# A block-attention and layer-norm kernel: three pair tiles and two single banks in PSUM, whole copies of the weight parts, sums in the keys' bank, and a new order of steps

## The chip, the cores and the metric

The kernel runs on one core of a Trainium2 chip. The core has five engines with a queue of instructions each: TensorE (PE, matmuls, with PEld for its weight loads), VectorE (DVE), ScalarE (ACT), GpSimd (POOL) and SyncE (SP, which issues the DMAs here). SBUF holds operands in 128 partitions; PSUM, where matmuls write, has eight banks of 128 x 512 floats. The metric is the device time of one execution in microseconds (us); lower is better.

## The reference

For each of 8 batches x is 512 x 1024 (float32). It is cut into 8 blocks of 64 rows. With q the second row of cond:

```
block  = sums of the 64 rows of each block            # 8 x 1024
keys   = block @ Wk.T, divided by their RMS, times rms_weight
attn   = softmax over the 8 blocks of keys . q
p      = (attn-weighted sum of block) @ Wo.T          # one row per batch
y      = x + p
out    = x + (y - mean(y)) / sqrt(var(y) + 1e-6) * gamma + beta
```

The residual in the last line is the input x, before p is added.

## The kernel before, in words

The 8 batches are four **groups** of two. A group's x comes in four tiles of 128 partitions x 2 rows x 1024, so there are 32 **rows** of 128 x 1024, named k = 0 to 31, eight to a group. Thirteen SBUF slots (x0 to x12) hold x tiles and, early on, the parts of Wk and Wo.

Per group: bs adds the blocks with matmuls against a 0/1 matrix (L417); col transposes the sums into columns (blkT, DVE, L427); proj.0 and proj.1 multiply them by the transposed Wk and Wo (L461, L447), which gives the keys and the values; the softmax (sm) is a chain of small steps on ACT, DVE, POOL and one small matmul, "sums" (L484 to L504); vw weights the values (L518); p spreads them over the partitions with eight matmuls (L533); two copies of 512 columns bring p into the SBUF tile pb (ACT L236, DVE L238). For group 0 the weights are transposed first: each part T is eight 128 x 128 transposes (L402) and two copies.

Per row k: S (DVE, L634) forms x + p in place with its sum, Q (ACT, L636) its squares' sum; a **unit** U of four rows (two at the very end) makes standard deviations and their reciprocals on POOL (v, std, s2, sd2, rs; the last units partly on ACT and DVE) and transposes small vectors (st, L709), which a copy brings into lt. D (DVE, L734) writes (gamma + std) times the row into PSUM; R (TensorE, L720) adds the rank-one terms of mean, p and beta from lt and a table, two rows at a time; E (ACT, L749) evicts the sum, scaled by the reciprocal deviation, back into x; SP stores it. Rows 30 and 31 are evicted in halves of 512 columns, one on ACT (L759) and one on DVE (L760).

PSUM is four tiles of two banks each, t0 to t3; a step's bank i lies in tile i // 2. Rows, weight parts and p each take a whole pair; sums, projections, st and block sums a single bank. A framework puts semaphores between instructions that touch the same tile, and takes a tile as a whole: an instruction that reads one bank of t3 waits for the last write into the other.

The order of work is written out by hand: every step has a number, and the string ORDER gives the numbers in the order in which they are issued, with a letter (a, b: which of the step's engines) and, after a colon, the bank or slot. "f n:bank" puts n **filler** matmuls of zeros into a bank (L848, nothing reads them; they also set the bank for a later D, whose matmul accumulates); "z" the same without start. Each engine works its own queue in that order.

## Time and profile before

| | us |
|---|---|
| runs, median of 3 | 156.93 (155.94 to 157.63) |
| profiled execution, its own time | 155.66 |
| its span (first to last instruction) | 153.9 |
| PE / DVE / ACT / POOL busy | 119.3 / 101.9 / 92.7 / 52.9 |
| mean granted clock of TensorE | 0.91 of 2.4 GHz |

The span is what the trace covers; 1.76 us of the execution's own time lie around it. The busy times are shares of stages with different limits; fillers are counted in PE's. A timeline row gives the start of an instruction, its length, the line, the operation and, in brackets, how long its engine stood idle before it and who ended that. Lengths in the timeline overlap a little at their ends, so instructions in a row start closer together than their lengths.

### The profile page before, as it was taken

What the parts mean: (1) busy time and instruction counts of PE and PEld (TensorE: products, weight loads), DVE (VectorE), ACT (ScalarE), POOL (GpSimd) and SP (SyncE); (2) the same over time, 40 slices, a digit from 0 to 9 for tenths busy, and PEclk for the clock granted to TensorE, in tenths of its full rate; (3) what the DMA queues carried; (4) which work ended last, traced back from release to release, by engine and by line L of the source; (5) the groups of instructions that cost most, each with busy time, mean ns of one, the idle gap of its engine ahead of it and who ended that gap; (6) DMA issues with size and microseconds to landing.
All of it is one profiled execution on the core that took longest, in us unless ns stands there. A gap on an engine that the chain in (4) does not pass through costs nothing.

```text
span 153.9 us, 3136 instructions
## 1 busy us (share of the span) xinstructions
PE 119.3 (77%) x1209; PEld 59.1 (38%) x1218; DVE 101.9 (66%) x181; ACT 92.7 (60%) x156; POOL 52.9 (34%) x88
## 2 busy tenths in 40 slices
PE   5978465799988998997695888896496898469660
PEld 2548255369654653443342313432241222212110
DVE  3022250317419996598999999678939999966940
ACT  3054211125414996648999968688589769967620
POOL 6882000000000261602087282259209326960000
PEclk9999999999999999999999559999689559779955
DMA  5999999999999980065999706246240752546793
GB/s 132 421 394 428 424 408 408 409 422 416 420 418 424 404 358 17 4 271 182 424 349 400 292 2 277 87 185 272 102 170 9 321 228 100 243 204 272 321 360 136
DMA packets 7671, 42.77 MB, mean 278 GB/s; under 512 B 824, under 2 KB 824, under 8 KB 3816
## 3 DMA queue, kind: packets, MB, share of 16 engines
q1 hardware_dynamic: 7584, 42.54, 68.7%
q8 instruction: 9, 0.15, 0.4%
q14 instruction: 6, 0.05, 0.1%
q10 hardware_dynamic: 72, 0.04, 0.1%
HBM read 25.73 MB, written 16.78 MB: 276 GB/s over the span
## 4 chain that ended last, share of the span: by engine, by line
PE 30%; DVE 29%; DMA 16%; ACT 10%; issue 7%; POOL 5%; ACTq 0%; DVEq 0%
DVE x L634 13%; DMA x<-in_x_dram 13%; DVE t L734 10%; PE t L461 7%; PE t L720 6%; ACT x L749 4%; PE t L417 4%; PE t L402 4%; DMA tab<-in_L_cond_ln_beta_dram 3%; PE t L533 3%; PE t L848 3%; PE t L447 3%; ACT pb L236 2%; POOL urs L703 1%; ACT square L636 1%
## 5 line engine op out<-in xcount | busy, mean ns | idle before, releaser
L734 DVE SCALAR_TENSOR_TENSOR t<-gam,ustd,x 128x1024 f32<-128x1024 f32 x32 | 40.5, 1287 | 7.5 <-ACT x L749 4.8
L636 ACT ACTIVATE square<-x,tot 128x1024 bf16<-128x1024 f32 x32 | 36.7, 1148 | 2.6 <-DVE x L634 2.2
L634 DVE SCALAR_TENSOR_TENSOR x<-x,pb 128x1024 f32<-128x1024 f32 x32 | 38.0, 1221 | 0.1
L749 ACT ACTIVATE x<-t,urs 128x1024 f32<-128x1024 f32 x30 | 32.5, 1107 | 6.8 <-PE t L720 3.8
L720 PE MATMUL t<-tab,lt 32*128 32x512 f32 x128 | 26.9, 750 | 3.5 <-ACT square L636 1.5
L848 PE MATMUL t<-zeros 128*128 128x512 bf16 x57 | 20.8, 483 | 10.4 <-DVE vw L518 2.9
L688 POOL TENSOR_SCALAR stat<-tot 128x8 f32<-128x8 f32 (+1 forms) x8 | 6.5, 813 | 61.4 <-DVE x L634 56.2
L417 PE MATMUL t<-x,blk 128*32 128x256 f32 x256 | 18.0, 414 | 3.1 <-DMA x<-in_x_dram 2.5
L402 PE MATMUL t<-ident,x 128*128 128x128 f32 x128 | 16.4, 282 | 4.2 <-DMA x<-in_L_cond_Wk_dram 2.6
L402 PEld LDWEIGHTS t<-ident,x 128*128 128x128 f32 x128 | 15.3, 193 | 6.4 <-issue 4.0
L461 PE MATMUL t<-wkT,blkT 128*32 128x256 f32 x256 | 15.4, 382 | 1.1 <-DVE blkT L427 0.6
L848 PEld LDWEIGHTS <-zeros 128*128 128x128 bf16 x66 | 6.8, 115 | 23.6 <-issue 20.2
L238 DVE COPY wkT<-t 128x512 f32<-128x512 f32 x7 | 4.7, 689 | 14.0 <-PE t L402 13.9
L720 PEld LDWEIGHTS t<-tab,lt 32*128 32x128 f32 x128 | 7.4, 210 | 16.2 <-issue 6.1
L461 PE MATMUL t<-woT,blkT 128*32 128x256 f32 x192 | 12.0, 382 | 1.8 <-ACT x L749 0.9
L236 ACT COPY wkT<-t 128x512 f32<-128x512 f32 x9 | 5.0, 588 | 13.5 <-PE t L402 12.4
L236 ACT COPY woT<-t 128x512 f32<-128x512 f32 x9 | 5.0, 585 | 11.9 <-DVE woT L238 6.9
L683 POOL TENSOR_TENSOR ustd<-uv,halfs 128x4 f32<-128x4 f32 (+1 forms) x8 | 11.6, 1453 | 1.2 <-ACT uv L679 0.7
L703 POOL TENSOR_TENSOR urs<-uv,halfs 128x4 f32<-128x4 f32 (+1 forms) x8 | 11.7, 1467 | 0.0
L417 PEld LDWEIGHTS t<-x,blk 128*32 128x32 f32 x256 | 7.6, 115 | 10.7 <-issue 3.3
L238 DVE COPY woT<-t 128x512 f32<-128x512 f32 x7 | 4.7, 688 | 10.4 <-ACT woT L236 5.4
L461 PEld LDWEIGHTS t<-wkT,blkT 128*32 128x32 f32 x256 | 7.6, 109 | 8.5 <-issue 1.3
(79 smaller groups left out, 96.7 us busy)
## 6 DMA issues: line engine op xcount, KB each, us to landing
x<-in_x_dram SPq DMA_DIRECT2D x16, 1024.0 KB
out_dram<-x SPq DMA_DIRECT2D x14, 1024.0 KB
x<-in_L_cond_Wk_dram SPq DMA_DIRECT2D x4, 1024.0 KB
x<-in_L_cond_Wo_dram SPq DMA_DIRECT2D x3, 1024.0 KB
x<-in_L_cond_Wo_dram SPq DMA_DIRECT2D x2, 512.0 KB
out_dram<-x SPq DMA_DIRECT2D x2, 512.0 KB
out_dram<-x SPq DMA_DIRECT2D x4, 256.0 KB
gam<-in_L_cond_ln_gamma_dram SPq DMA_DIRECT2D x1, 512.0 KB
```

The lines of the kernel that those rows point to most:

```text
L236: nc.scalar.copy(dst, src)
L402: nc.tensor.transpose(flat(pair(part))[:, bass.ts(c, P)], tile_of(name)[:, e % RT, c::HC], ident)
L417: nc.tensor.matmul(bank(f"bs{n}")[32 * j : 32 * j + 32, :QU], blk[G["g"]], tile_of(name)[:, r, bass.ts(j, QU)], start=(t == 0 and r == 0), ...
L461: nc.tensor.matmul(bank(name)[32 * j : 32 * j + 32, :QU], b[:, c, :], w[:, c, j], start=(c == 0), stop=(c == HC - 1),)
L634: add(f"S{k}", [(DVE, 1.15)], lambda e: nc.vector.scalar_tensor_tensor(x_row(k), x_row(k), 1.0, pb[n], ALU.mult, ALU.add, accum_out=total) ...
L636: add(f"Q{k}", [(ACT, 1.28)], lambda e: nc.scalar.activation(square, x_row(k), AF.Square, bias=total, scale=-float(H), accum_out=ssq), rea ...
L683: add(f"{T} std", [(POOL, 0.5 + 0.16 * U)], lambda e: nc.gpsimd.tensor_tensor(std, v, halfs[:, :1].to_broadcast([P, U]), ALU.pow), reads=[ ...
L703: add(f"{T} rs", [(POOL, 0.5 + 0.16 * U)], lambda e: nc.gpsimd.tensor_tensor(rs, v, halfs[:, 1:].to_broadcast([P, U]), ALU.pow), reads=[V, ...
L720: nc.tensor.matmul(pair(f"row{k}")[:, h, :], lts[q % NST][lo : lo + 32, r // RT, :], tab_of(k)[0][lo : lo + 32, :], start=False, stop=True ...
L734: add(f"D{k}", [(DVE, 1.21)], lambda e: nc.vector.scalar_tensor_tensor(flat(pair(name)), gam, std, x_row(k), ALU.add, ALU.mult), reads=["g ...
L749: add(f"E{k}", [(ACT, 1.13)], lambda e: nc.scalar.activation(x_row(k), flat(pair(name)), AF.Identity, scale=rs), reads=[RS], writes=[xk(k) ...
L848: nc.tensor.matmul(banks[i // 2][:, i % 2, :], zeros, zeros[:, 0:1].to_broadcast([P, HALF]), start=start, stop=True, skip_group_check=True)
```

## The change

PSUM becomes three pair tiles (t0 to t2, banks 0 to 5) and two single ones (b0 and b1, banks 6 and 7). A step of the new kind "P" takes two banks that may lie in two tiles: p of each group, the weight part T1.7 and row 31. The other weight parts are copied by one instruction of 1024 columns. The softmax's sums go into columns 256 to 271 of the keys' bank, and that bank is held until the scores (sc) are taken. Row 31 has its own D, R and E per half; row 30 is evicted whole and stored as one piece. There is a filler of 256 columns ("h"). ORDER is new: the softmax of group 2 stands earlier, the scaling of gam goes to ACT, two more of the lt copies go to DVE, there are 81 fillers in place of 66, and two x tiles swap slots.

```diff
@@ -28,6 +28,7 @@
 FORMS = ('y',)
-SPLIT = (30, 31)
+SPLIT = (31,)
+APART = ((1, 7),)
 ALONE = (30, 31)
 UP = 32768.0
-SINGLE = (28, 29)
+SINGLE = (28, 29, 30)
 POOL_UNITS = (0, 1, 2, 3, 4, 5, 6, 7)
@@ -42,24 +43,24 @@
 ORDER = (
-    "1 3 45:0 84 2 4 0 46:1 87 75 5 86 47:2 6 82 7 48:3 8 9 10 11 12 14 13 15 16 17 18 19 20 21 22 23 24 f11:7 "
...
+    "1 3 45:0 84 2 4 75 46:1 92 5 0 79 47:2 6 80 7 48:3 8 9 10 11 12 14 13 15 16 17 18 19 20 21 22 23 24 f11:7 "
...
 )
@@ -104,6 +105,6 @@
         for word in order.split():
-            if word[0] in "fz":
+            if word[0] in "fhz":
                 count, bank = map(int, word[1:].split(":"))
                 for _ in range(count):
-                    unread(bank, word[0] == "f")
+                    unread(bank, word[0] == "f", 256 if word[0] == "h" else 512)
                 if word[0] == "f":
@@ -118,3 +119,3 @@
                     unset.add(at)
-                elif kind == "t":
+                elif kind in "tP":
                     for i in (at, at + 1):
@@ -180,11 +181,16 @@
     wT = [alloc("wkT", [P, HC, H]), alloc("woT", [P, HC, H])]
-    banks = [ps.tile([P, 2, HALF], F32, tag=f"t{s}", name=f"t{s}") for s in range(4)]
+    pairs = [ps.tile([P, 2, HALF], F32, tag=f"t{s}", name=f"t{s}") for s in range(3)]
+    singles = [ps.tile([P, HALF], F32, tag=f"b{s}", name=f"b{s}") for s in range(2)]
+
+    def bank_at(i):
+        return pairs[i // 2][:, i % 2, :] if i < 6 else singles[i - 6]
 
     def bank(name):
+        return bank_at(plan.at[name])
 
-        i = plan.at[name]
-        return banks[i // 2][:, i % 2, :]
+    def half(name, i):
+        return bank_at(plan.at[name] + i)
 
     def pair(name):
-        return banks[plan.at[name] // 2]
+        return pairs[plan.at[name] // 2]
 
@@ -401,8 +407,15 @@
             for c in range(HC):
-                nc.tensor.transpose(flat(pair(part))[:, bass.ts(c, P)], tile_of(name)[:, e % RT, c::HC], ident)
-        add(f"{part} mm", [(PE, 1.22)], lambda _: go(), reads=[f"{name}.{e % RT}", "ident"], claim=("t", part), release=name)
+                nc.tensor.transpose(half(part, c // 4)[:, bass.ts(c % 4, P)], tile_of(name)[:, e % RT, c::HC], ident)
+        apart = (which, e) in APART
+        add(f"{part} mm", [(PE, 1.22)], lambda _: go(), reads=[f"{name}.{e % RT}", "ident"],
+            claim=("P" if apart else "t", part), release=name)
         dst = wT[which][:, :, e * P : (e + 1) * P]
+        if not apart:
+            add(f"{part} cp", [(ACT, 1.08), (DVE, 1.25)], lambda en: copy(
+                en, dst, flat(pair(part)).rearrange("p (c k) -> p c k", c=HC)),
+                reads=[("slot", part)], writes=[f"wt{which}.{e}.{i}" for i in range(2)], release=[part, part])
+            return
         for i in range(2):
             add(f"{part} cp{i}", [(ACT, 0.6), (DVE, 0.69)], lambda en, i=i: copy(
-                en, dst[:, 4 * i : 4 * i + 4, :], pair(part)[:, i, :].rearrange("p (c k) -> p c k", c=4)),
+                en, dst[:, 4 * i : 4 * i + 4, :], half(part, i).rearrange("p (c k) -> p c k", c=4)),
                 reads=[("slot", part)], writes=[f"wt{which}.{e}.{i}"], release=part)
@@ -487,3 +500,3 @@
             kw, bank(keys)[:, :QU], 1.0, qw, ALU.mult, ALU.mult, accum_out=sd[:, 1:2]),
-            reads=["qw"], writes=["sd1"], use=keys, release=keys)
+            reads=["qw"], writes=["sd1"], use=keys)
         add(f"{T} sdd", [(DVE, 0.2), (POOL, 0.6)], lambda e: engine[e].tensor_tensor(
@@ -491,10 +504,10 @@
             reads=["sd0", "sd1", "diag8"], writes=["sdd"])
-        pc = f"sums{n}"
+        at = slice(QU, QU + 2 * NBLK)
         add(f"{T} mm", [(PE, 0.3)], lambda e: nc.tensor.matmul(
-            bank(pc)[:, : 2 * NBLK], mask, flat(sdd), start=True, stop=True), reads=["sdd", "mask"], claim=("b", pc))
-        add(f"{T} v", [(DVE, 0.18)], lambda e: nc.vector.tensor_scalar(cv, bank(pc)[:, :NBLK], 1.0 / H, EPS, ALU.mult, ALU.add),
-            writes=["cv"], use=pc)
+            bank(keys)[:, at], mask, flat(sdd), start=True, stop=True, skip_group_check=True), reads=["sdd", "mask"], use=keys)
+        add(f"{T} v", [(DVE, 0.18)], lambda e: nc.vector.tensor_scalar(cv, bank(keys)[:, QU : QU + NBLK], 1.0 / H, EPS, ALU.mult, ALU.add),
+            writes=["cv"], use=keys)
         inverse_root(T, cv, c0, ca, ca, ("cv", "c0", "ca", "ca"))
         add(f"{T} sc", [(DVE, 0.18)], lambda e: nc.vector.scalar_tensor_tensor(
-            cs, bank(pc)[:, NBLK : 2 * NBLK], -1.0, ca, ALU.mult, ALU.mult), reads=["ca"], writes=["cs"], use=pc, release=pc)
+            cs, bank(keys)[:, QU + NBLK : QU + 2 * NBLK], -1.0, ca, ALU.mult, ALU.mult), reads=["ca"], writes=["cs"], use=keys, release=keys)
         add(f"{T} mx", [(DVE, 0.18)], lambda e: nc.vector.tensor_reduce(mx, cs, AX.X, ALU.min), reads=["cs"], writes=["mx"])
@@ -521,6 +534,6 @@
 
-        add(f"{part} mm", [(PE, 1.0)], lambda e: spread_p(G, part, True), reads=[f"vw{n % 2}", f"spread{g}"], claim=("t", part))
+        add(f"{part} mm", [(PE, 1.0)], lambda e: spread_p(G, part, True), reads=[f"vw{n % 2}", f"spread{g}"], claim=("P", part))
         for i in range(2):
             add(f"{part} cp{i}", [(ACT, 0.6), (DVE, 0.69)], lambda e, i=i: copy(
-                e, bands(pb[n % 2])[:, :, i, :], pair(part)[:, i, :].rearrange("p (q d) -> p q d", d=P)),
+                e, bands(pb[n % 2])[:, :, i, :], half(part, i).rearrange("p (q d) -> p q d", d=P)),
                 reads=[("slot", part)], writes=[f"pb{n % 2}.{i}"], release=part)
@@ -533,3 +546,3 @@
                 nc.tensor.matmul(
-                    pair(part)[:, i, :].rearrange("p (q j d) -> p j q d", j=2, d=HB)[:, j], spread[g][lo, j, :],
+                    half(part, i).rearrange("p (q j d) -> p j q d", j=2, d=HB)[:, j], spread[g][lo, j, :],
                     vw[n % 2][lo, :].rearrange("p (q d) -> p q d", d=HB),
@@ -720,3 +733,3 @@
         nc.tensor.matmul(
-            pair(f"row{k}")[:, h, :], lts[q % NST][lo : lo + 32, r // RT, :], tab_of(k)[0][lo : lo + 32, :],
+            half(f"row{k}", h), lts[q % NST][lo : lo + 32, r // RT, :], tab_of(k)[0][lo : lo + 32, :],
             start=False, stop=True, skip_group_check=True)
@@ -754,3 +767,3 @@
 
-        _, _, rs, RS, _ = reads_of(k)
+        std, D, rs, RS, reads = reads_of(k)
         name = f"row{k}"
@@ -758,6 +771,14 @@
             cols = slice(h * HALF, (h + 1) * HALF)
+            add(f"D{k}.{h}", [(DVE, 0.66)], lambda e, h=h, cols=cols: nc.vector.scalar_tensor_tensor(
+                half(name, h), gam[:, cols], std, x_row(k)[:, cols], ALU.add, ALU.mult),
+                reads=["gam", D, xk(k)] + ([f"{name}.at"] if h else []), writes=[f"{name}.{h}"] + ([] if h else [f"{name}.at"]),
+                claim=None if h else ("P", name))
+        for h in range(2):
+            add(f"R{k}.{h}", [(PE, 0.5)], lambda e, h=h: outer(k, h), reads=reads, writes=[f"{name}.{h}"])
+        for h in range(2):
+            cols = slice(h * HALF, (h + 1) * HALF)
             add(f"E{k}.{h}", [(ACT, 0.68), (DVE, 0.69)], lambda e, h=h, cols=cols: nc.scalar.activation(
-                x_row(k)[:, cols], pair(name)[:, h, :], AF.Identity, scale=rs) if e == ACT else nc.vector.tensor_scalar(
-                x_row(k)[:, cols], pair(name)[:, h, :], rs, None, ALU.mult),
-                reads=[("slot", name), RS], writes=[f"out{k}.{h}"], release=name)
+                x_row(k)[:, cols], half(name, h), AF.Identity, scale=rs) if e == ACT else nc.vector.tensor_scalar(
+                x_row(k)[:, cols], half(name, h), rs, None, ALU.mult),
+                reads=[f"{name}.{h}", RS], writes=[f"out{k}.{h}"], release=name)
 
@@ -768,2 +789,6 @@
             some = ks[at : at + n]
+            if some[0] in SPLIT:
+                halves(some[0])
+                store(some[0])
+                continue
             for k in some:
@@ -772,6 +797,3 @@
             for k in some:
-                if k in SPLIT:
-                    halves(k)
-                else:
-                    finish(k)
+                finish(k)
                 store(k)
@@ -845,6 +867,6 @@
 
-    def unread(i, start):
+    def unread(i, start, n=HALF):
 
         nc.tensor.matmul(
-            banks[i // 2][:, i % 2, :], zeros, zeros[:, 0:1].to_broadcast([P, HALF]), start=start, stop=True,
+            bank_at(i)[:, :n], zeros, zeros[:, 0:1].to_broadcast([P, n]), start=start, stop=True,
             skip_group_check=True)
```

DVE, its queue at the first results, before (t, x, lt: tiles with their numbers; L486 and L489 belong to the softmax of group 1, L734 is a D, L427 a col):

```order
L486 SCALAR_TENSOR_TENSOR kw_116,sd_117<-t3_81,qw_96 128x256
L489 TENSOR_TENSOR sdd_118<-diag8_88,sd_117 128x16
L347 TENSOR_SCALAR gam_97<-gam_97 128x1024
L734 SCALAR_TENSOR_TENSOR t0_78<-gam_97,ustd0_150,x1_64 128x1024
L495 TENSOR_SCALAR cv_119<-t3_81 128x8
L734 SCALAR_TENSOR_TENSOR t1_79<-gam_97,ustd0_150,x1_64 128x1024
L427 STREAM_TRANSPOSE blkT0_100<-t2_80 128x256
```

and in the changed kernel (lines are 13 higher there):

```order
L499 SCALAR_TENSOR_TENSOR kw_117,sd_118<-t0_78,qw_97 128x256
L502 TENSOR_TENSOR sdd_119<-diag8_89,sd_118 128x16
L440 STREAM_TRANSPOSE blkT0_101<-t2_80 128x256
L747 SCALAR_TENSOR_TENSOR t1_79<-gam_98,ustd0_151,x1_64 128x1024
L508 TENSOR_SCALAR cv_120<-t0_78 128x8
L244 COPY lt0_99<-t2_80 128x256
L747 SCALAR_TENSOR_TENSOR t2_80<-gam_98,ustd0_151,x1_64 128x1024
```

The scaling of gam has left the queue, col of group 2 stands ahead of the first D instead of behind the second, and a copy of lt out of t2 stands between the two D.

DVE around the first S of the last group (row 24, in x11), before (L238 is a half copy of p into pb1):

```order
L518 TENSOR_SCALAR vw1_103<-t3_81,wcol_125 128x256
L734 SCALAR_TENSOR_TENSOR t1_79<-gam_97,ustd0_150,x5_68 128x1024
L634 SCALAR_TENSOR_TENSOR x10_73,tot1_94<-x10_73,pb0_104 128x1024
L238 COPY pb1_105<-t0_78 128x4x128
L634 SCALAR_TENSOR_TENSOR x11_74,tot0_93<-x11_74,pb1_105 128x1024
L734 SCALAR_TENSOR_TENSOR t0_78<-gam_97,ustd0_150,x7_70 128x1024
```

and in the changed kernel:

```order
L531 TENSOR_SCALAR vw1_104<-b1_82,wcol_126 128x256
L747 SCALAR_TENSOR_TENSOR t0_78<-gam_98,ustd0_151,x7_70 128x1024
L747 SCALAR_TENSOR_TENSOR t1_79<-gam_98,ustd1_152,x10_73 128x1024
L647 SCALAR_TENSOR_TENSOR x11_74,tot0_94<-x11_74,pb1_106 128x1024 x2
L747 SCALAR_TENSOR_TENSOR t2_80<-gam_98,ustd1_152,x10_73 128x1024
```

Both halves of pb1 are copied by ACT now, two D stand between vw and the S of row 24, and 21 D are ahead of that S where 18 were.

DVE at the end, before (L760 evicts a half):

```order
L734 SCALAR_TENSOR_TENSOR t0_78<-gam_97,ustd0_150,x6_69 128x1024
L238 COPY lt0_98<-t3_81 128x128
L734 SCALAR_TENSOR_TENSOR t2_80<-gam_97,ustd0_150,x6_69 128x1024
L760 TENSOR_SCALAR x6_69<-t0_78,urs0_142 128x512
L760 TENSOR_SCALAR x6_69<-t2_80,urs0_142 128x512
```

and in the changed kernel (L772 is a half D):

```order
L747 SCALAR_TENSOR_TENSOR t2_80<-gam_98,ustd0_151,x6_69 128x1024
L772 SCALAR_TENSOR_TENSOR b0_81<-gam_98,ustd0_151,x6_69 128x512
L772 SCALAR_TENSOR_TENSOR b1_82<-gam_98,ustd0_151,x6_69 128x512
L781 TENSOR_SCALAR x6_69<-b0_81,urs0_143 128x512
```

The last D is in two pieces in two tiles, the lt copy is ACT's, and DVE evicts one half where it evicted two.

## Rows read from the trace of the kernel before

**Rows 1.** The profile page, busy time of each engine (us, share of the span, instructions).

```profile
PE 119.3 (77%) x1209; PEld 59.1 (38%) x1218; DVE 101.9 (66%) x181; ACT 92.7 (60%) x156; POOL 52.9 (34%) x88
```

**Rows 2.** The chain of waits at the head: start, length, engine and line.

```profile
42.88 0.91 PE t L417 x16
...
43.81 0.49 DVE vw L518
...
44.44 1.16 PE t L533 x8
...
46.96 2.38 DVE x L634 x4
```

**Rows 3.** Timeline of DVE: start, length, instruction, [idle before it and who ended it].

```profile
57.04 0.69 DVE L347 TENSOR_SCALAR gam<-gam 128x1024 f32<-128x1024 f32 x1
59.24 1.29 DVE L734 SCALAR_TENSOR_TENSOR t<-gam,ustd,x 128x1024 f32<-128x1024 f32 x1 [1.52 <-PE t L848]
...
63.41 0.17 DVE L503 RECIPROCAL es<-es 128x1 f32<-128x1 f32 x1 [0.46 <-ACT cs L501]
...
65.43 3.68 DVE L734 SCALAR_TENSOR_TENSOR t<-gam,ustd,x 128x1024 f32<-128x1024 f32 x3 [1.06 <-remote]
...
72.50 1.29 DVE L734 SCALAR_TENSOR_TENSOR t<-gam,ustd,x 128x1024 f32<-128x1024 f32 x1 [0.34 <-ACT x L749]
...
91.10 1.29 DVE L734 SCALAR_TENSOR_TENSOR t<-gam,ustd,x 128x1024 f32<-128x1024 f32 x1 [0.35 <-ACT x L749]
...
98.53 1.29 DVE L734 SCALAR_TENSOR_TENSOR t<-gam,ustd,x 128x1024 f32<-128x1024 f32 x1 [1.13 <-ACT x L749]
100.97 0.42 DVE L486 SCALAR_TENSOR_TENSOR kw<-t,qw 128x256 bf16<-128x256 f32 x1 [1.14 <-ACT square L484]
...
104.13 0.17 DVE L495 TENSOR_SCALAR cv<-t 128x8 f32<-128x8 f32 x1 [0.43 <-PE t L461]
...
114.21 0.69 DVE L238 COPY pb<-t 128x512 f32<-128x512 f32 x1 [2.35 <-ACT pb L236]
```

**Rows 4.** The same timeline of DVE, from 130 us to the end.

```profile
132.88 0.41 DVE L238 COPY lt<-t 128x256 f32<-128x256 f32 x1
...
137.21 1.29 DVE L734 SCALAR_TENSOR_TENSOR t<-gam,ustd,x 128x1024 f32<-128x1024 f32 x1 [1.41 <-ACT x L749]
...
141.45 1.29 DVE L734 SCALAR_TENSOR_TENSOR t<-gam,ustd,x 128x1024 f32<-128x1024 f32 x1 [1.41 <-ACT x L749]
...
145.05 1.28 DVE L734 SCALAR_TENSOR_TENSOR t<-gam,ustd,x 128x1024 f32<-128x1024 f32 x1
147.08 0.75 DVE L760 TENSOR_SCALAR x<-t,urs 128x512 f32<-128x512 f32 x1 [0.75 <-ACT x L759]
148.91 0.75 DVE L760 TENSOR_SCALAR x<-t,urs 128x512 f32<-128x512 f32 x1 [1.07 <-PE t L720]
```

**Rows 5.** The page's costliest groups: busy us, mean ns of one, idle before.

```profile
L734 DVE SCALAR_TENSOR_TENSOR t<-gam,ustd,x 128x1024 f32<-128x1024 f32 x32 | 40.5, 1287 | 7.5 <-ACT x L749 4.8
...
L634 DVE SCALAR_TENSOR_TENSOR x<-x,pb 128x1024 f32<-128x1024 f32 x32 | 38.0, 1221 | 0.1
L749 ACT ACTIVATE x<-t,urs 128x1024 f32<-128x1024 f32 x30 | 32.5, 1107 | 6.8 <-PE t L720 3.8
```

**Rows 6.** Timeline of PE: row matmuls and fillers at either clock.

```profile
113.47 1.14 PE L720 MATMUL t<-tab,lt 32*128 32x512 f32 x8
114.55 1.48 PE L848 MATMUL t<-zeros 128*128 128x512 bf16 x6
...
121.00 2.72 PE L848 MATMUL t<-zeros 128*128 128x512 bf16 x6 [0.46 <-ACT lt L236]
123.65 2.09 PE L720 MATMUL t<-tab,lt 32*128 32x512 f32 x8
```

**Rows 7.** By stage: window, its us, busy of each engine, PEclk, DMA share, GB/s.

```profile
83.00:105.00 22.00, 18.50 (x196) 7.57 (x201) 18.84 (x29) 17.67 (x30) 10.74 (x11) 0.84 0.43 177
105.00:125.00 20.00, 14.94 (x68) 5.56 (x61) 17.30 (x28) 15.83 (x25) 9.03 (x8) 0.78 0.50 206
```

42 rows, old and new, of the table ORDER are left out of this document.

## The prediction, made before the changed kernel ran

> **What bounds the kernel now.** I read the page's busy times first. No engine is full [rows 1]: DVE works 101.9 of 153.9 us, and TensorE's 119.3 us hold filler matmuls that nobody reads. So the end is set by hand-offs, and I went to the chain of waits. Up to 46.96 us it runs through the loads and the attention of group 0; there the first S (x+p on DVE) starts, behind block sums, weighting, p matmul and copies [rows 2]. From that S to DVE's last instruction, which ends at 149.66 (148.91 + 0.75) [rows 4], DVE is the spine: 32 S of 1.22 us and 32 D of 1.29 us [rows 5], which follow each other every 1.15 and 1.20 us in a row of them, one D in the run of three of 3.68 us [rows 3] being about 1.2.
>
> The timeline of DVE then shows where the spine stands still. The waits of rows 3 and 4 add up to 13.4 us of the 102.7 between 46.96 and 149.66. In the order of the program:
> - 1.52, 0.46, 1.06 and 0.34 at the first results (59 to 73 us): 3.38;
> - 0.35, 1.13, 1.14 and 0.43 from 91 to 104 us: 3.05, three of the four ended by ACT;
> - 2.35 before the last group's p copy (114.21), the longest;
> - 1.41 and 1.41 late, both ended by an eviction E on ACT; then 0.75 and 1.07 between the last evictions.
>
> The other thing to see is TensorE's clock. Its stages from 83 to 125 us have a mean granted clock of 0.84 and 0.78 [rows 7], a mixture of the levels 2.4 and 1.2 GHz: the same eight row matmuls take 1.14 us at the one and 2.09 at the other, six fillers 1.48 and 2.72 [rows 6].
>
> **The change, part by part.** I replayed the new order by hand, each step with its duration from the rows, full clock, and every hand-off at once.
>
> *Head.* vw of group 0 starts at 43.81, right after the block sums that end at 43.79 (42.88 + 0.91) [rows 2]. These write another bank of the same tile t3, which is what the weighting reads. With p0 after it, that is one line: sums, vw 0.49, p. After the change the values lie in t0 and the sums in t1, so vw runs beside the sums and p can start at 43.9 instead of 44.44. The two p halves now lie in separate tiles, but both copies write the one pb tile and still follow each other. First S: **-0.6**, at 46.4.
>
> *One copy per part.* Fifteen whole copies stand for thirty halves. No row has one; bounds are 1.11 us on ACT (E, also 1024 columns from PSUM, rows 5) and 2 x 0.69 on DVE (two half copies as at 114.21, rows 3). They are hidden under the loads and the transposes; the last part, T1.7, keeps its halves. Zero; if the cover fails, some 0.2 us each for the last three.
>
> *Sums in the keys' bank.* The same matmul into other columns: no cost by itself. The keys' bank is held until the scores are taken, a few us longer; who wants it next is the next projection, and that one has b0, b1 and one half of a pair to choose from. Bounds 0 to +0.5; I take 0.
>
> *First results.* The scaling of gam (0.69 [rows 3]) leaves DVE for ACT; the columns of group 2 (0.44, much like the 0.42 for 256 columns at 100.97 [rows 3]) come ahead of D0. D0 can start when these are done, at about 57.75 instead of 59.24. But it is paid back: D1 writes t2, whose fillers stand on TensorE behind the transposes of the first unit; those too lie in t2, and are read by a copy that DVE makes itself (lt, 0.41 [rows 4]). I find 0.65 us for the copy's wait, 1.2 before D1, 0.5 and 0.25 behind it, and 0.25 before the columns: 2.85 against 3.38: **-0.5**. Bounds: +1.2 (D1 takes two fillers at half clock and D2 the same) and -1.5.
>
> *91 to 104 us.* Scores and weighting of group 2 now stand in front of S8 to S15 instead of among them, and what follows of groups 2 and 3 has room: ACT has no late square of the keys (it ended the 1.14) and fewer evictions queued when DVE comes. In the replay no wait over 0.2 is left. All is -3.05; none is 0, if the waits only move on, since their ends are on ACT. I take **-2.5**.
>
> *p of the last group.* Before, p3 wants t0, a pair that also carries rows, and stands on TensorE behind four fillers and a unit's transposes; the wait is 2.35. Now it has b0 and b1, and while p (1.16 [rows 2]) and two copies run, DVE has two D (2.4) to do: **-2.3**. Bounds -2.35 and -1.2 (a half-clock p and one copy late). In the replay S24 starts at 113.3 with 21 D done; before, at 114.9 (114.21 + 0.69) with 18. Three D at 1.2 and 1.6 make 5.2 us ahead, against 5.0 for the terms so far with the added work below: the check on them.
>
> *The end.* Before, 4.05 us pass from the end of the last D (145.05 + 1.28) to the last eviction on ACT, which follows DVE's (149.66) by one eviction of half a row, about 0.7. Row 31 now goes in halves through b0 and b1, each with its own D, R and E; row 30 is evicted whole on ACT beside them. After the last half D: R of a half (0.57, half of 1.14 [rows 6]), E 0.75 [rows 4], about 1.4 us. **-2.6**; the two half D's cost 0.15 more than one whole (each 0.72, between half a D, 0.64, and 0.75 for 512 columns). Bounds -1.3 (E30 on ACT, 1.11, in the way of the last E) and -2.7.
>
> *The two waits of 1.41.* They hang on evictions that come late from statistics on POOL and row matmuls at half clock. With the work further ahead I count half: **-1.0** (0 to -2.8).
>
> *More work on DVE.* Three more lt copies of 256 columns [rows 4] for one of 128 less (about 0.3): +0.9; three small ones of the softmax that leave POOL, 0.17 each [rows 3]: +0.5; row 31: +0.15; gam: -0.69. **+0.9**.
>
> The sum: -0.6 - 0.5 - 2.5 - 2.3 - 2.6 - 1.0 + 0.9 = -8.6. That is a replay with perfect hand-offs; the clock will not allow it. Two row pairs at half clock that show (2 x 0.95) and 0.2 of small waits take back 2.1: **-6.5**. The profiled execution took 155.66 us (span 153.9), 1.27 below the median of the runs; from there 149.2, and at the median's level 156.93 - 6.5 = **150.4**.
>
> **A rule that speaks against the change.** Rows first: TensorE falls to 1.2 GHz in the stretches that follow its waits, and the stage of 105 to 125 us, with 14.94 us busy of 20, has 0.78 [rows 7]. The change spreads fillers over more banks and tiles, 81 instead of 66. The Trainium skill, page "TensorE: Matmul & The Clock Gate", section "A second HAM failure mode: psum-queue depth-cycling", says that a kernel that cycles through PSUM banks with small idle times between its matmul groups had its clock swing between the levels. By it the fillers would not hold the clock, and the sum would come out as in the third rival; by the rows, waits of TensorE shrink with DVE's, and half-clock time should not grow.
>
> **Rivals.**
> 1. *All hand-offs hold.* Nothing taken back: about 148.3; with all bounds at the good end (-0.6, -1.5, -3.05, -2.35, -2.7, -2.8, +0.9 = -12.1) 145. For: every term has its row. Against: before shows 13.4 us of waits in an order as carefully written.
> 2. *The waits only move.* Of the eight longest, five are ended by ACT, and ACT has as much left behind S24 (a dozen evictions of 1.11, eight squares of about that length, copies and small ones: some 25) as DVE (8 S, 10 D, two halves, copies and small ones: 25.4). Then only the head, half of p's 2.3 and 1.3 of the end stay, less +0.9 work and +1.2 at the first results: -1.0, **155.9**, no change. The singles are then right and the order buys nothing.
> 3. *Slower: TensorE at 1.2 GHz from about 85 us on.* From there to the end run nine pairs of rows. A pair at half clock costs TensorE 2.09 + 2.72 for six fillers = 4.8 us [rows 6]; DVE spends 2 x 1.15 + 2 x 1.20 = 4.7 on one. TensorE then sets the pace, with unit transposes on top, and the ten small fillers ahead of row 18 and each longer queue lie in front of the row matmul. It decides when R lands later than ACT's slot for E, under 1 us of slack. Nine pairs by 0.95 is 8.6: it eats the gain and the 2.1 already counted rise to some 10, **159**. For: the mean of 0.78 before [rows 7]. Against: a mean of 0.78 is a mixture, so the clock was not kept down for good, and a busier DVE feeds TensorE more steadily.
>
> **How the numbers follow.** A difference under about 1% (1.6 us) can't be told from none. The forecast (148 to 153.5) gets 0.50; rival 1 (under 148) 0.13; a partial gain between the forecast and rival 2 (153.5 to 155.4) 0.11; rival 2 0.14; rival 3 and slower mishaps like it 0.12. Faster 0.74, same 0.14, slower 0.12. The range of 8 in 10 goes from 146 (a third of rival 1 below it) to 157 (rival 3 and a little of rival 2 above it).
>
> **What would show it.** First S at 46.2 to 46.6 and vw of group 0 within 0.1 of the last values matmul: the head. D0 before 58.2, then waits of about 1 before D1: first results. No wait of DVE over 0.5 between 80 and 113: the order. S24 at 113 to 115 with 21 D done: p3. From the last half D to the last eviction under 2 us: the end. Wrong it would be if DVE's waits still add to over 11 us, if the granted clock from 105 to the end lies below 0.7, or if row matmuls of about 2.1 us stand for most pairs after 85 us.

## The result, and the profile after

The changed kernel takes 149.88 us (median of 4 runs, 148.11 to 150.64) against 157.28 for the kernel before on the same occasions: a ratio of 0.952 (95% interval 0.938 to 0.966). The profiled execution took 148.11 us, its span 146.4 us, 7.5 less than before. The forecast was 150.4 us, in a range of 146 to 157. Some runs of every kernel are a few per cent longer than its others: the ratios here and below leave out those over 1.5% above its fastest, the medians don't.

The page of the changed kernel: busy time of each engine, then DVE's two groups of long instructions (busy us, mean ns of one, idle before them):

```profile
PE 118.9 (81%) x1226; PEld 60.5 (41%) x1233; DVE 102.6 (70%) x180; ACT 90.3 (62%) x143; POOL 48.2 (33%) x87
...
L747 DVE SCALAR_TENSOR_TENSOR t<-gam,ustd,x 128x1024 f32<-128x1024 f32 x31 | 39.1, 1286 | 3.1 <-remote 1.1
...
L647 DVE SCALAR_TENSOR_TENSOR x<-x,pb 128x1024 f32<-128x1024 f32 x32 | 37.8, 1216 | 0.3 <-ACT pb L242 0.2
```

DVE does as much as before (102.6 against 101.9 us [rows 1]); what went are its waits: 3.1 us stand ahead of the D instead of 7.5 [rows 5]. Its timeline, the rows that answer to [rows 3, 4]:

```profile
43.98 0.69 DVE L244 COPY pb<-b 128x512 f32<-128x512 f32 x1 [1.41 <-PE b L546]
44.76 1.23 DVE L647 SCALAR_TENSOR_TENSOR x<-x,pb 128x1024 f32<-128x1024 f32 x1
...
55.98 0.42 DVE L499 SCALAR_TENSOR_TENSOR kw<-t,qw 128x256 bf16<-128x256 f32 x1 [1.63 <-ACT square L497]
...
57.81 0.45 DVE L440 STREAM_TRANSPOSE blkT<-t 128x256 f32<-128x256 f32 x1 [1.19 <-PE t L430]
58.22 1.29 DVE L747 SCALAR_TENSOR_TENSOR t<-gam,ustd,x 128x1024 f32<-128x1024 f32 x1
...
61.88 1.29 DVE L747 SCALAR_TENSOR_TENSOR t<-gam,ustd,x 128x1024 f32<-128x1024 f32 x1 [1.12 <-remote]
...
72.93 1.23 DVE L647 SCALAR_TENSOR_TENSOR x<-x,pb 128x1024 f32<-128x1024 f32 x1 [0.23 <-ACT pb L242]
...
114.34 1.22 DVE L647 SCALAR_TENSOR_TENSOR x<-x,pb 128x1024 f32<-128x1024 f32 x1
...
135.42 1.29 DVE L747 SCALAR_TENSOR_TENSOR t<-gam,ustd,x 128x1024 f32<-128x1024 f32 x1 [0.64 <-ACT x L762]
...
138.82 1.42 DVE L772 SCALAR_TENSOR_TENSOR b<-gam,ustd,x 128x512 f32<-128x512 f32 x2
140.79 0.75 DVE L781 TENSOR_SCALAR x<-b,urs 128x512 f32<-128x512 f32 x1 [0.55 <-PE b L733]
```

Between 75 and 133 us no wait of DVE is over 0.25 us. Before S24 (114.34) the two D that stand there run without a break: the 2.35 us are gone. And from 83 to 115 us TensorE kept its clock where it had lost it before, while from 125 to 135 us it lost more (0.67 against 0.84); windows of the changed kernel and then of the kernel before (us, busy of each engine, PEclk, the granted clock as a share of 2.4 GHz, third from the end):

```profile
83.00:95.00 12.00, 8.65 (x64) 3.41 (x63) 12.00 (x18) 11.61 (x18) 7.76 (x8) 1.00 0.80 274
...
105.00:115.00 10.00, 8.11 (x51) 3.62 (x45) 9.30 (x18) 8.56 (x15) 4.11 (x7) 1.00 0.65 264
...
125.00:135.00 10.00, 8.12 (x30) 2.95 (x32) 8.94 (x13) 8.54 (x13) 7.29 (x6) 0.67 0.75 304
```

```profile
83.00:95.00 12.00, 9.47 (x68) 3.50 (x73) 11.54 (x18) 9.97 (x17) 6.25 (x6) 0.72 0.54 224
...
105.00:115.00 10.00, 6.89 (x41) 2.99 (x35) 7.30 (x17) 7.47 (x13) 3.99 (x4) 0.83 0.51 210
...
125.00:135.00 10.00, 7.18 (x32) 2.27 (x29) 9.72 (x14) 8.63 (x12) 7.68 (x8) 0.84 0.39 158
```

So the number came out. Whether the reasons did is another matter. The change is two things, an order and tiles. The sum credits 4.9 us to the places where p and row 31 use the two single tiles, and 4.6 to the order and the placing of steps (0.6, 0.5, 2.5 and 1.0).

### The profile page after: what moved, and what is told of

The parts are those of the page before. It is cut to its first block, busy times and chain, and to the rows that moved or that the text cites. A ratio compares the mean times of both kernels' runs of the same rounds, so it can differ in the third digit from the quotient of the medians.

```text
span 146.4 us, 3140 instructions
## 1 busy us (share of the span) xinstructions
PE 118.9 (81%) x1226; PEld 60.5 (41%) x1233; DVE 102.6 (70%) x180; ACT 90.3 (62%) x143; POOL 48.2 (33%) x87
## 4 chain that ended last, share of the span: by engine, by line
DMA 30%; PE 27%; DVE 23%; ACT 6%; POOL 5%; issue 5%; another core or an unknown queue 1%; POOLq 0%; DVEq 0%; ACTq 0%; SPq 0%
DMA x<-in_x_dram 22%; DVE t L747 12%; DVE x L647 8%; PE b L474 6%; DMA out_dram<-x 5%; PE t L474 4%; PE t L733 4%; PE t L408 3%; DMA tab<-in_L_cond_ln_gamma_dram 3%; ACT x L762 3%; PE t L430 3%; ACT square L649 3%; POOL mask L286 2%; PE b L430 1%; PE b L733 1%
## 5 line engine op out<-in xcount | busy, mean ns | idle before, releaser
L870 PE MATMUL b<-zeros 128*128 128x512 bf16 (+1 forms) x60 | 17.6, 419 | 3.3 <-DVE zeros L295 2.1
L408 PE MATMUL t<-ident,x 128*128 128x128 f32 x120 | 14.9, 278 | 4.5 <-DMA x<-in_L_cond_Wk_dram 3.0
L430 PE MATMUL t<-x,blk 128*32 128x256 f32 x192 | 12.6, 384 | 3.6 <-DMA x<-in_x_dram 3.6
L242 ACT COPY wkT<-t 128x1024 f32<-128x1024 f32 x4 | 3.9, 1016 | 14.9 <-PE t L408 14.9
L474 PE MATMUL b<-wkT,blkT 128*32 128x256 f32 x192 | 11.4, 381 | 0.8 <-DVE blkT L440 0.7
L244 DVE COPY woT<-t 128x1024 f32<-128x1024 f32 x4 | 4.9, 1220 | 7.7 <-PE t L408 7.7
L244 DVE COPY wkT<-t 128x1024 f32<-128x1024 f32 x4 | 4.7, 1219 | 6.8 <-PE t L408 6.8
L430 PEld LDWEIGHTS t<-x,blk 128*32 128x32 f32 x192 | 5.2, 109 | 10.2 <-DMA x<-in_x_dram 6.7
L474 PEld LDWEIGHTS b<-wkT,blkT 128*32 128x32 f32 x192 | 6.1, 109 | 4.8 <-issue 1.9
L474 PE MATMUL b<-woT,blkT 128*32 128x256 f32 x128 | 7.9, 381 | 0.0
```

What stands on the lines that cost most here:

```text
L244: engine[e].tensor_copy(dst, src)
L408: nc.tensor.transpose(half(part, c // 4)[:, bass.ts(c % 4, P)], tile_of(name)[:, e % RT, c::HC], ident)
L430: nc.tensor.matmul(bank(f"bs{n}")[32 * j : 32 * j + 32, :QU], blk[G["g"]], tile_of(name)[:, r, bass.ts(j, QU)], start=(t == 0 and r == 0), ...
L474: nc.tensor.matmul(bank(name)[32 * j : 32 * j + 32, :QU], b[:, c, :], w[:, c, j], start=(c == 0), stop=(c == HC - 1),)
L870: nc.tensor.matmul(bank_at(i)[:, :n], zeros, zeros[:, 0:1].to_broadcast([P, n]), start=start, stop=True, skip_group_check=True)
```

## The experiments

**Order and tiles apart.** Two kernels, each with one half of the change.

```diff
 # e1: the changed kernel, banks 6 and 7 one tile
-    pairs = [ps.tile([P, 2, HALF], F32, tag=f"t{s}", name=f"t{s}") for s in range(3)]
-    singles = [ps.tile([P, HALF], F32, tag=f"b{s}", name=f"b{s}") for s in range(2)]
+    pairs = [ps.tile([P, 2, HALF], F32, tag=f"t{s}", name=f"t{s}") for s in range(4)]
...
-        return pairs[i // 2][:, i % 2, :] if i < 6 else singles[i - 6]
+        return pairs[i // 2][:, i % 2, :]
```

```diff
 # e2: the kernel before, banks 6 and 7 two tiles
-    banks = [ps.tile([P, 2, HALF], F32, tag=f"t{s}", name=f"t{s}") for s in range(4)]
+    banks = [ps.tile([P, 2, HALF], F32, tag=f"t{s}", name=f"t{s}") for s in range(3)]
+    singles = [ps.tile([P, HALF], F32, tag=f"b{s}", name=f"b{s}") for s in range(2)]
...
+        return banks[i // 2][:, i % 2, :] if i < 6 else singles[i - 6]
```

> The changed kernel, its order and steps untouched, but banks 6 and 7 are again one tile of two banks (t3), so that every reader or writer of the one waits for the other. Theory A (order and tiles each take away other waits of DVE): the waits of the old kernel between 91 and 104 us stay away, the copies of p and the row-31 halves are bound to each other again: 151 to 152.5 us. Theory B (the two single tiles are what pays): back to within 1% of the kernel before, 156 to 158. Theory C (the order is what pays): as the changed kernel, 149.3 to 150.5.

> The kernel before, its order and steps untouched, but banks 6 and 7 are two single tiles. Theory A: the weighting of group 0 no longer waits for the block sums of group 1 and small hand-offs in these banks come free, the waits from 91 to 104 us, the 2.35 us before the last group's p and the end stay: 155 to 156.5 us. Theory B: most of the gain, 150 to 152. Theory C: as the kernel before, 156.5 to 158.

Measured: e1 156.63 us (ratio 0.995, 0.988 to 1.002), e2 147.96 us (0.941, 0.933 to 0.949), and the changed kernel once more beside them 148.76 us (0.949, 0.943 to 0.956).

> The changed kernel once more, beside the three others on the same chip: 149 to 150.5 us; its profile shows whether half-clock stretches sit at 125 to 140 us again (0.78 in the first profile).

The half-clock stretch was there again: from 125 to 140 us the granted clock is 0.73 in this profile, 0.78 in the first.

Theory B, with both ends: the new order on the old tile, for which it was not written, is worth nothing, the old order on the new tiles is worth all of it; e2 is no slower than the changed kernel (the intervals overlap). My theory A falls. Whole copies, the sums in the keys' bank and the other parts of the order were not run one by one; all together they leave no gain over e2. In the profile of e1 the waits are back, in other places (DVE's timeline):

```profile
98.30 2.49 DVE L746 SCALAR_TENSOR_TENSOR t<-gam,ustd,x 128x1024 f32<-128x1024 f32 x2 [2.91 <-PE t L869]
...
119.51 1.23 DVE L646 SCALAR_TENSOR_TENSOR x<-x,pb 128x1024 f32<-128x1024 f32 x1 [1.83 <-ACT pb L241]
```

and in e2 DVE has no wait over 0.5 us from 66 to 129 us, with not one step moved. So the waits of [rows 3] from 91 to 114 us, of which the rows put four down to ACT and one to PE, came from the shared tile. TensorE's timeline shows how. The kernel before:

```profile
84.84 0.44 PE L709 MATMUL t<-ident,stat 128*128 128x128 f32 x2
85.87 1.94 PE L417 MATMUL t<-x,blk 128*32 128x256 f32 x16 [0.59 <-ACT lt L236]
87.74 2.09 PE L720 MATMUL t<-tab,lt 32*128 32x512 f32 x8
...
109.58 0.58 PE L848 MATMUL t<-zeros 128*128 128x512 bf16 x1 [2.88 <-DVE vw L518]
```

and e2:

```profile
84.02 0.44 PE L712 MATMUL b<-ident,stat 128*128 128x128 f32 x2
84.54 1.07 PE L420 MATMUL b<-x,blk 128*32 128x256 f32 x16
...
103.17 0.81 PE L851 MATMUL b<-zeros 128*128 128x512 bf16 x2 [0.57 <-DVE cs L501]
```

At 85 us the block sums (bank 6) wait for ACT to copy the transposes out of bank 7; at 107 us three fillers for bank 7 wait for DVE's weighting, which reads bank 6. Without the shared tile the first wait is not there and the second is 0.57. In the kernel before, TensorE had just waited 1.76 us for p; during the further 0.59 its clock fell to 1.2 GHz (0.50 from 86 to 92 us), and the block sums took 1.94 instead of 1.07 us.

The engine that the rows name was itself held. ACT's timeline before, at the waits of 98 and 101 us:

```profile
97.11 0.37 ACT L236 COPY lt<-t 128x256 f32<-128x256 f32 x1 [1.29 <-PE t L461]
...
100.46 0.38 ACT L484 ACTIVATE square<-t 128x256 bf16<-128x256 f32 x1 [0.83 <-PE t L461]
```

The lt copy waits for a quarter of the keys, the square of the keys for matmuls of the values, each in the other bank. In e2 these two instructions wait 0.18 and 0.27 us.

**Which of the waits.** Three kernels put some of them back into e2, by fillers in the other bank or by reads of one unused column (some 0.2 us each).

```diff
 # e7: e2, fillers into the bank that lt is copied from (ORDER)
-    ... f6:7 403 ... f1:6 466 ... f1:7 472 ... f2:6 516 ...
+    ... f6:6 403 ... f1:7 466 ... f1:6 472 ... f2:7 516 ...
```

```diff
 # e8: e2, group 3 alone: one-column reads ahead of sq, v, sc and unit 3's lt copy
+        copy(ACT, square[:, 0:1], bank("proj3.1")[:, 500:501])   # ahead of sq
+        copy(DVE, cv[:, 0:1], bank("proj3.1")[:, 500:501])       # ahead of v
+        copy(DVE, cs[:, 0:1], bank("proj3.1")[:, 500:501])       # ahead of sc
+        copy(ACT, lt[:, 0:1], bank("proj3.0")[:, 500:501])       # ahead of lt
```

```diff
 # e9: e2, block sums behind unit 2's lt copy; fillers behind the weighting
+        copy(ACT, square[:, 0:1], bank("bs3")[:, 500:501])       # behind lt of unit 2
-    ... 441b f3:7 ...
+    ... 441b f3:6 ...
```

e11 is e8 and e9 together, with one more read of the keys' bank behind unit 3's lt copy. e8 and e9 also have one more filler each, in bank 6, and e11 has both.

> The old order with the two single tiles (148.0 in the run before), but four groups of late fillers (six ahead of rows 20 and 21, one each ahead of rows 24 and 26, two ahead of row 31) go into the bank from which a unit's transposes are being copied to lt, so that they wait for that copy as they did when banks 6 and 7 were one tile. Theory F (the shared tile cost its time by holding TensorE's fillers, and with them the row matmuls and the clock, behind the lt copies): 151 to 154. Theory G (it cost its time in the attention of the last group, where keys and values lay in one tile): 147.5 to 148.7.

> The old order with the two single tiles, but with four reads of one unused column added (some 0.2 us each) that bring back the waits of the old tile in the last group's attention alone: the lt copy of unit 3 waits for the first quarter of the keys, the square of the keys and the two readers of the sums wait for the values' matmuls, and these for the readers. Theory G: the waits at 98, 101 and 104 us come back and with them half the gain or more, 152 to 155. Theory F: 148.0 to 149.2 (the added reads alone, at most 0.8).

> The old order with the two single tiles (148.0), with two of the old tile's waits put back on purpose: the second block sums of the last group wait again for unit 2's lt copy (through one added read of an unused column on ACT, some 0.2 us), and the three fillers behind the last group's weighting go into the bank that the weighting reads, so that they wait for it. In the kernel before, TensorE stood idle 0.59 us at 85 us and 2.88 us at 107 us by these two, and its clock fell to 1.2 GHz right after each. Theory H (the shared tile costs most of its time through the clock, by two small waits of TensorE that add to longer ones): half-clock stretches at 85 to 92 and 109 to 113 us come back, 150.5 to 154. Theory I (the clock falls for other reasons and the waits are only worth their length on DVE): 148.0 to 149.0.

> The two waits of the run before together with the waits in the last group's attention (149.9 by themselves): six waits of the old tile between 85 and 109 us, tiles still single. If these six are what the shared tile cost, 154 to 157; if they only add, 150.5 to 152; the rest of the 8.7 us would then lie in waits outside this stretch.

| kernel | us, median of 6 | lowest to highest | ratio to the kernel before |
|---|---|---|---|
| e2, the waits gone | 147.96 | 145.64 to 148.60 | 0.941 (0.933 to 0.949) |
| e7, fillers behind lt | 148.18 | 147.23 to 149.69 | 0.952 (0.944 to 0.960) |
| e8, keys and values | 149.86 | 147.62 to 151.28 | 0.959 (0.947 to 0.972) |
| e9, the two waits of TensorE | 149.47 | 148.44 to 151.14 | none on record |
| e11, e8 and e9 | 152.79 | 152.17 to 154.11 | none on record |

e7 brings 0.2 us by its median, and its interval overlaps e2's; theory F, which wanted 3 us or more, falls. e8 and e9 bring some 1.9 and 1.5 us, each less than its theory wanted and at the edge of the spread; both at once 4.8, more than their sum and clear of it (e11's fastest run is 3.6 us above e2's slowest). That is over half of the 8.7 us between e2 and the kernel before. The other 3.9 is in couplings of the tile that I did not put back one by one, and stays open.

DVE's timelines say which waits of [rows 3] come back. In e8 they are 0.40, 0.92 and 0.43 us at 95, 98 and 101 us (1.13, 1.14 and 0.43 before), in e9 2.05 us ahead of the last group's p copy (2.35 before), and in e11 all four:

```profile
97.29 1.29 DVE L740 SCALAR_TENSOR_TENSOR t<-gam,ustd,x 128x1024 f32<-128x1024 f32 x1 [0.93 <-ACT x L755]
99.92 0.42 DVE L491 SCALAR_TENSOR_TENSOR kw<-b,qw 128x256 bf16<-128x256 f32 x1 [1.33 <-ACT square L489]
...
103.08 0.16 DVE L242 COPY cv<-b 128x1 f32<-128x1 f32 x1 [0.43 <-PE b L465]
...
113.52 0.69 DVE L242 COPY pb<-t 128x512 f32<-128x512 f32 x1 [2.54 <-ACT pb L240]
```

So these rows are the shared tile's, the 2.35 us ahead of p included: they return with the old order, single tiles and p still in t0. On the clock, e9's TensorE, with ACT's added read ahead of it:

```profile
83.90 0.18 ACT L239 CAST square<-b 128x1 bf16<-128x1 f32 x1
...
85.36 1.94 PE L420 MATMUL b<-x,blk 128*32 128x256 f32 x16 [1.88 <-DMA x<-in_x_dram]
87.22 2.09 PE L724 MATMUL t<-tab,lt 32*128 32x512 f32 x8
...
106.24 0.81 PE L852 MATMUL b<-zeros 128*128 128x512 bf16 x2 [2.89 <-DVE vw L521]
...
107.82 2.08 PE L536 MATMUL t<-vw,spread 64*128 64x256 f32 x8
```

The second wait, and the half-clock p behind it, are those of the kernel before (2.88 us; the granted clock from 105 to 115 us is 0.83 in both). The first is not: the added read ends at 84.08, and the block sums start 1.3 us later, when a load lands. So the half-clock stretch at 85 us is no sign for theory H, and only the second wait was tested. e11's profile has late loads too: TensorE waits 1.44 and 3.22 us for them, and DVE 1.27 behind the second, which is not the tile's. In e11 the clock stayed at 1.00 from 83 to 105 us, and DVE's waits at 97 to 103 us are there all the same: such waits cost without a fall of the clock.

**The fillers.** From the changed kernel, 51 fillers in banks 6 and 7 behind the first results are left out (ten of them of 256 columns).

```diff
-    ... f2:7 ... f3:7 ... f3:7 ... f3:6 ... h10:7 ... f6:7 ... f6:7 ... f3:6 ... f2:6 ... f4:7 ...
+    ...
```

> The changed kernel without the 51 fillers in the two single banks that stand behind the first eight results (the few that set a bank for row 31 come back by themselves). If fillers keep TensorE at 2.4 GHz here, the granted clock from 83 to 125 us falls from 1.00 and 0.99 to 0.8 or lower, row matmuls of 2.1 us become common, and the time rises to 151 to 155. If waits of DVE are all that counts, TensorE has less to do and the time stays at 148.5 to 150.

Measured 155.86 us (ratio 1.001, 0.996 to 1.006): the whole gain is gone. Its windows:

```profile
83.00:95.00 12.00, 8.31 (x48) 3.10 (x44) 11.86 (x18) 11.27 (x17) 7.19 (x7) 0.51 0.79 273
...
125.00:135.00 10.00, 5.24 (x17) 1.47 (x19) 9.09 (x13) 8.07 (x13) 8.77 (x8) 0.50 0.52 212
135.00:145.00 10.00, 9.05 (x21) 2.57 (x23) 5.37 (x12) 7.33 (x13) 0.97 (x1) 0.50 0.69 281
```

TensorE sits at 1.2 GHz for most of that stretch (granted clock 0.71 from 83 to 125 us, 0.50 behind it), and the time lies above the 151 to 155 expected. This is the third rival's state; it costs 7 us by the medians, where the rival had 8.6. The fillers are what kept the changed kernel out of it.

**The head.** The first S is made later by repeating a copy.

```diff
             add(f"{part} cp{i}", [(ACT, 0.6), (DVE, 0.69)], lambda e, i=i: [copy(
                 e, bands(pb[n % 2])[:, :, i, :], half(part, i).rearrange("p (q d) -> p q d", d=P))
+                for _ in range(3 if n == 0 and i == 0 else 1)],
```

> The changed kernel with the first S made later on purpose: DVE's half copy of group 0's p is made three times over, some 1.2 us more on DVE before the first S, which then starts at about 46.0 instead of 44.8. If the head behind the first eight S is held by what still has to be loaded (the last tile of group 2's x and gamma, both landing at about 57 us), the wait of 1.63 us behind S7 takes it up and the time stays within 0.3 us of the changed kernel. If DVE's own chain from the first S is what counts, the time rises by 1.0 to 1.3 us.

Measured 150.02 us (148.51 to 151.71), beside 148.76 (147.25 to 153.52) for the changed kernel: the median is 1.3 higher, as if DVE's chain counted, but the ranges lie in each other: the times don't decide. The profiles say more. The first S starts at 44.76, 46.12 and 46.33 us in the first profile of the changed kernel, its second and e3's, and S8 at 72.93, 71.92 and 72.09: an early first S is not kept. In the first profile the scaling of gamma on ACT begins at the moment gamma lands (ACT's timeline):

```profile
57.04 1.06 ACT L352 ACTIVATE gam<-gam 128x1024 f32<-128x1024 f32 x1 [1.10 <-DMA gam<-in_L_cond_ln_gamma_dram]
```

and no D can start before that is done, 58.1. In e3 the weighting of group 0 starts as early as in that profile (42.20 and 42.09), the first S 1.57 us later, and the first D at 57.36 instead of 58.22: there the delay cost nothing.

**The end.** Row 31 whole in the changed kernel (e6), and in halves in the old order with new tiles (e10).

```diff
 # e6: D of row 31 whole into a pair, both R in one step, evictions out of the pair
-                half(name, h), gam[:, cols], std, x_row(k)[:, cols], ALU.add, ALU.mult),
+                flat(pair(name)), gam, std, x_row(k), ALU.add, ALU.mult),   # h == 0 only
```

```diff
 # e10: e2, row 31 in halves through banks 6 and 7
-            flat(pair(name)), gam, std, x_row(k), ALU.add, ALU.mult), ...
+            flat(pair(name)), ... if k < 31 else [nc.vector.scalar_tensor_tensor(bank_at(6 + h), ...) for h in range(2)], ...
...
-    ... 515:4 510 493 511a 512b f2:6 516 ...
+    ... 515:6 510 493 511a 512b 516 ...
```

> The changed kernel with row 31 whole again: one D into a pair tile, both row matmuls, then two evictions out of that pair; the filler between the two row matmuls is left out. My term for the end was -2.6 us, of which the profile of the changed kernel showed 1.2 (2.85 us from the last D to the last eviction's end instead of 4.05). If the halves are what brought it, the last two evictions follow each other again and the time rises by 0.7 to 1.3, to 149.5 to 150.5; if it came from row 30 being evicted whole, it stays at 148.8.

> The old order with the two single tiles, and row 31 in halves through them as in the changed kernel (two fillers ahead of its row matmul left out); row 30 stays evicted in two halves. If two readers of one tile waiting for each other is what separates the last two evictions (the second began 0.03 us after the first ended, in every profile with a whole row 31), they run beside each other and the time falls by 0.5 to 1.0, to 147.0 to 147.5; if the end is set by the row matmul or the store, it stays at 148.0.

e6: 149.49 us (148.13 to 153.07), not told apart from the changed kernel. e10: 146.63 us (ratio 0.944, 0.937 to 0.951), by its median 1.3 below e2, by its ratio not told apart from it (0.941). The last evictions show the step itself; e6 on ACT (the other half's, on DVE, ran from 142.00 to 142.75), then e10 on ACT (DVE's from 141.43 to 142.17):

```profile
142.79 0.69 ACT L780 ACTIVATE x<-t,urs 128x512 f32<-128x512 f32 x1 [0.87 <-DVE x L781]
```

```profile
141.12 0.69 ACT L764 ACTIVATE x<-b,urs 128x512 f32<-128x512 f32 x1 [0.39 <-PE b L723]
```

Two readers of one pair wait for each other; two readers of two singles don't. In the trace that is one eviction of half a row, some 0.7 us; no time shows it clearly. From the end of the last D to the end of the last eviction it is 3.47 us in e2 and 2.34 in e10, but 2.70 in e6 against 2.85 and 4.72 in the two profiles of the changed kernel: there the last row matmul, at half clock, decides.

**More fillers.** e12 is e10 with twelve more, ahead of row 18, unit 6 and unit 7.

```diff
-    ... f6:7 382 ... f4:6 462:7 ... f3:7 485:6 ...
+    ... f11:7 382 ... f8:6 462:7 ... f6:7 485:6 ...
```

> The old order with single tiles and row 31 in halves (146.6), with 12 more fillers in three places where TensorE waits over 1 us: five ahead of rows 18 and 19, four ahead of unit 6's transposes, three ahead of unit 7's. If these waits are what lets the clock fall at 112 and at 126 us, it stays at 2.4 GHz longer, row matmuls at 131 us take 1.1 instead of 2.1 us, and the time falls to 144.8 to 146.2. If fillers stand in front of work that is wanted, 146.8 to 148.

Measured 146.30 us (145.40 to 148.19), the span of the profile 144.3, the mean granted clock 0.97 (e10: 0.924), and 1.00 in every window from 95 to 135 us, where e10 has 0.50 from 128 to 132:

```profile
125.00:135.00 10.00, 7.28 (x37) 2.54 (x40) 8.54 (x14) 8.07 (x12) 5.94 (x6) 1.00 0.51 211
```

The clock did as expected; the time lies between the two ranges and is not told from e10's. e10 and e12 are the fastest kernels here by their medians, some 10 us below the kernel before and 2 to 3 below the changed one: old order, two single tiles, row 31 in halves. Against the changed kernel that is not clear of the spread (ratios to the kernel before 0.944 for e10 and 0.949 for the changed kernel, whose intervals overlap).

## Why the prediction was right, and where not

- **The sum.** Forecast -6.5, measured -7.4 by the medians. The rival "the waits only move" and the slower one did not come.
- **The step that failed: what the order is worth.** I took -2.5 for the waits from 91 to 104 us as the work of the new order, with the argument that it leaves ACT, which ends three of the four, more room. e2 removes them with no step moved, e1 keeps waits of 2.91 and 1.83 with every step moved. ACT was only the last one named; what held it was a matmul in the other bank, and with those waits put back (e8, e11) DVE's return. The p of the last group (-2.3, measured -2.35) has the same cause: e2 has no wait there either, with p still in t0, and e9, which holds three fillers behind the weighting, has 2.05 us. Rival 2, in which the singles are right and the order buys nothing, came to 1.0 us in all; the singles alone brought 8.7.
- **First S.** Forecast 46.4; 44.76 and 46.12. I said the two p copies still follow each other since both write pb; they begin at 43.98 on DVE and 44.02 on ACT. It was the common PSUM tile that bound them. From the end of the values' matmuls to the first S it is 4.08 us before and 2.75 in both profiles, -1.3 where I had -0.6; the rest of the difference is when the values end (42.88 before, 42.01 and 43.37). The early start is not kept: no D can start before gamma has landed and is scaled.
- **First results.** D0 at 58.22 (forecast 57.75), the waits at D1 and behind it 0.77, 1.12, 0.69 and 0.39 against 0.65, 1.2, 0.5 and 0.25. S8 came at 72.93. The waits behind D0 held (2.97 us, forecast 2.6), the saving did not: with the two waits ahead of D0 (1.63 and 1.19) that an early first S turns into, DVE stands 5.8 us there, 3.4 in the second profile, against 2.85 forecast and 3.38 before.
- **S24** at 114.34 with 21 D done; the replay had 113.3.
- **The end.** Forecast -2.6; from the last D's end (140.24) to the last eviction's (143.09) it is 2.85 instead of 4.05: -1.2. TensorE was in part at half clock there (1.36 us for the last half's row matmul) and had a filler between the two halves of R: the second eviction on ACT began at 142.40, 1.6 after DVE's. In the second profile that matmul takes 2.07 us and the whole stretch is 4.72, more than the 4.05 of the kernel before. The mis-sized part is R of the last half, which I had at 0.57 us, full clock; that two single tiles let both evictions run side by side, e10 shows.
- **The two waits of 1.41** became 0.84 and 0.64: -1.3 (forecast -1.0). **DVE's work** rose by 0.7 (forecast 0.9).
- **The clock.** I added 2.1 for half-clock time that a replay misses. The mean granted clock rose from 0.91 to 0.961 in the first profile, 0.934 in the second. I had taken the section of the Trainium skill, page "TensorE: Matmul & The Clock Gate", on cycling through PSUM banks ("A second HAM failure mode: psum-queue depth-cycling") to speak against the change. It names small idle times between groups of matmuls, and falls came behind waits of TensorE here too (the 2.88 us at 107 us before); but fillers over more banks went with a higher clock, not a lower one, and without 51 of them it was 0.80.

The forecast's size came from adding up DVE's waits, which was sound; for about half of the sum its reasons stood for the wrong half of the change, and that it came out is in this part luck. The same waits would have gone by either reading, so the number could not tell.

## What to carry to other kernels

Where a framework tracks dependencies by whole tiles, give each PSUM bank that is used by itself a tile of its own before reordering anything; compare the waits of every instruction with and without, since a profile names the engine that came last and not the tile that bound it. An engine that is not the bottleneck (here TensorE) is worth following one step further: its short waits held the copies and evictions that DVE waited for, and where its clock fell behind them, its matmuls took up to twice as long. When a change has two parts, cost each part alone against the rows, and run each alone.

## What was not expected of the hardware

Two engines that only read the same PSUM tile were serialized in these programs (ACT's last eviction began 0.04 us after DVE's ended in e6), and ran side by side out of two tiles (43.98 and 44.02 us). Leaving out 51 matmuls that nobody reads, of 0.25 us or less each at full clock, made the kernel 7 us slower. The same kernel's first S moved by 1.4 us between two executions (44.76 and 46.12) while its S8 moved by 1.0 the other way.
